# Layer 0's attention steps: two maxima over two banks, the sum of quotients and depthwise on VectorE, the norm on ScalarE

## The chip, the cores and the metric

The kernel runs on one core of a Trainium2 chip. The metric is the device time of one execution in microseconds, as the median of several runs. A core has TensorE (matrix products, its result goes to PSUM, a memory of eight banks for each of 128 partitions), VectorE, ScalarE, GpSimd (which does not take part in PSUM here), SyncE and DMA queues. Each engine works through its own list of instructions in order, and waits at an instruction until what it needs is there.

## What is computed

The reference is a stack of four layers, each with a residual and a group norm before it. Only layer 0 is touched here, on eight images of 128 channels and 56 x 56 pixels:

```python
x = x + L0(gn(x))                      # then layers 1 to 3
# L0, for each image, in 7 x 7 windows of 8 x 8 pixels:
proj = xw @ W_qkv + b_qkv              # q, k, v of 128 channels each
q_win, k_win = q.mean(pixels), k.mean(pixels)
logit = einsum('npc,nqc->npq', q_win * SCALE, k_win)
r_idx = top_k(logit, 4)                # four windows are chosen for each window
attn = softmax(einsum('bmqc,bmkc->bmqk', q_h * SCALE, k_sel))   # 8 heads of 16
o = attn @ v_sel
lepe = depthwise_3x3(v_img) + lepe_b
out = (o + lepe) @ W_o + b_o
```

## The kernel before

All eight images stay on chip as `X`. Layer 0 has 8 x 49 windows; two at a time make a pair, and the 196 pairs are worked off in a pipeline of steps, one loop iteration `p` each, in an order that is written out by hand for TensorE, VectorE, ScalarE and GpSimd. The order within a step is a list of names, `SHORT`, or `LONGER` for a step that also holds a depthwise job.

In step `p` these parts stand on a pair's way, pair `p + 2` entering while pair `p` leaves:

- `scores(p + 2)` (TensorE): the products of the queries, with one head of each two masked, and the chosen keys, for both windows (`o`) and four groups of channels (`g`), into one bank of PSUM for each group (`s0` to `s3` in the pool `ps_s`).
- `maxima` (VectorE, line 577): four, one for each group over 2 x 256 columns, giving the negated maximum of each row. `halve` (GpSimd) splits the result in two bf16 numbers, `flip` (TensorE) turns it, into bank `t2`, and `flipped` (ScalarE) copies it to `nm`.
- `shifted(p + 1)` (TensorE, lines 602 and 612): the transposed scores, four banks `t0` to `t3`; it begins with a product with `nm`, which subtracts the maxima. `exp0` to `exp3` (ScalarE, line 622) make the exponentials.
- `values(p)` (TensorE, line 636): exponentials times values, into bank `s0`. It can only start when `max0` of this step has freed that bank, and the next `scores` needs it back.
- `turned` and `divide` (VectorE, lines 648 to 660) read `values`' result and divide by the sum, into `ot`.
- `join(p - 2)` (GpSimd, line 465): adds the depthwise result to the quotients of the pair before the last. `back(p - 2)` (VectorE, line 471) turns the sum into `outs`.
- `gather` (GpSimd, line 534) copies the chosen keys, `fetch` issues DMAs of the chosen values.

Beside this, each step has room for two jobs, `one` (bank `t0`) and `two` (bank `t1`), and a small one, `light`. A job has a part for TensorE and an end on ScalarE or VectorE. Jobs are `queries` (q, ends on ScalarE, line 415), `keys`, `image` and `pixels` (k and v of the next image, end on ScalarE), `depthwise` (ends on VectorE, lines 449 and 451, and has its input `v` brought by `neighbours`, four DMAs on GpSimd's queue, line 429) and `project` (the output product; ends on VectorE, line 487, with the residual). A planner places them: each has a first step (`ready`) and a last one (`due`), and the earliest due goes first; in a step with depthwise, that is `two`, and it uses bank `t0`. In `SHORT` the end of `one` stands between `exp2` and `exp3`, the end of `two` after `flipped`.

The norm of the next image is done block by block, 49 times in layer 0's loop, in a step's `hooks` at its end, by four instructions of VectorE each (line 292). `hooks` also hold statistics (lines 226 and 496) and sums (line 297), which the planner spreads by weights.

Of the kernel before, what the change touches and what calls it, by code (L numbers as in the profile page):

```python
# [50 lines left out]
def conv_stack_kernel(ctx: ExitStack, tc: tile.TileContext, a: dict, out: bass.AP):  # L51
# [81 lines left out]
    with ExitStack() as l0:  # L133
# [69 lines left out]
        banks = itertools.cycle([(ps, f"{k}{g}") for k, ps in (("s", ps_s), ("t", ps_t)) for g in range(4)])  # L203
# [14 lines left out]
        def measure(b):  # L218
# [28 lines left out]
            def first_root():  # L247

                sd = small.tile([P, 1], F32, name="sd0", tag="sd1")
                nc.scalar.activation(sd, st["pv"], AF.Sqrt, bias=eps)  # L250
                st["r"] = small.tile([P, 1], F32, name="r0_0", tag="r0", bufs=4)
                nc.vector.reciprocal(st["r"], sd)
                st["off"] = small.tile([P, 1], F32, name="off", tag="off", bufs=1)
                nc.vector.tensor_scalar(st["off"], st["gm"], st["r"], -1.0, ALU.mult, ALU.mult)

            def var_end():


                v, t = (small.tile([P, 1], F32, name=f"nr{k}_{b}", tag=f"nr{k}") for k in range(2))
                y = st["r"] = small.tile([P, 1], F32, name=f"r0_{b}", tag="r0", bufs=4)  # L260
                nc.vector.tensor_scalar(v, st["pv"], EPS, None, ALU.add)
                nc.vector.tensor_scalar(t.bitcast(I32), v.bitcast(I32), 1, None, ALU.logical_shift_right)
                nc.vector.tensor_scalar(
                    y.bitcast(I32), t.bitcast(I32), -1.0, float(0x5F3759DF), ALU.mult, ALU.add
                )
                for c in (3.0, 12.0, 768.0):
                    nc.vector.scalar_tensor_tensor(t, y, v, y, ALU.mult, ALU.mult)
                    nc.vector.scalar_tensor_tensor(y, t, -c, y, ALU.add, ALU.mult)
                nc.vector.tensor_scalar(y, y, -1.0 / 8192, None, ALU.mult)

# [188 lines left out]
        def join(p):  # L459


            to = pairs[p]["ot"].rearrange("p k h (q c) -> p k (h q) c", c=FEW)
            for s in sorted({2 * p // NW, (2 * p + 1) // NW}):
                x = lepes[s][:, :, p - s * NW // 2].rearrange("p m (k c) -> p k m c", c=FEW)
                nc.gpsimd.tensor_tensor(to, to, x, ALU.add)
# [93 lines left out]
        def scores(p):  # L559
# [3 lines left out]
                s=[ps_s.tile([P, 2, TOPK * WPX], F32, name=f"s_{p}_{g}", tag=f"s{g}") for g in range(4)],  # L563
                nmax=win.tile([P, 2, 4], F32, name=f"nmax_{p}", tag="nmax"),
            )
            for o in range(2):
                w = wins[2 * p + o]
                for g in range(4):
                    h = slice(g * CL, (g + 1) * CL)
                    nc.tensor.matmul(  # L570
                        s_["s"][g][:, o, :], w["qm"][h].rearrange("p h x -> p (h x)"), w["kw"][h],
# [3 lines left out]
        def maxima(p, g):  # L575
            s_ = pairs[p]
            nc.vector.tensor_reduce(s_["nmax"][:, :, g], s_["s"][g], AX.X, ALU.max, negate=True)  # L577
# [72 lines left out]
        def divide(p):  # L650
# [8 lines left out]
            ot = pairs[p]["ot"] = win.tile([P, 4, 2, 16], F32, name=f"ot_{p}", tag="ot", bufs=2)  # L659
# [12 lines left out]
        made, jobs, hooks, fixed, loose = {}, [], {}, [], []  # L672
# [57 lines left out]
        for f in (image[0], image[1], *pixels[1:]):  # L730
# [3 lines left out]
                     light=(ps_s, "s2"), tails=(ps_s, "s1"))  # L734
# [9 lines left out]
        hook(-1, lambda: neighbours(0, 0))  # L744
# [10 lines left out]
        for b in range(B):  # L755
            for i in range(NBLK):
                q, last = pair_of(b, i * NW), pair_of(b, i * NW + NW - 1)
                if b or i > 1:
                    job(max(pair_of(b, i * NW - NW - 1) - 1, -1), q - 3, lambda b=b, i=i: queries(b, i))
                job(q + 1, q + 1, lambda b=b, i=i: depthwise(b, i), True, LONG)  # L760
                job(last + 3, last + 5, lambda b=b, i=i: project(b, i), name=("project", b, i))
        for b in range(1, B):
# [15 lines left out]
            for i in range(NBLK):  # L778
                fixed.append((at[i], 7, lambda b=b, i=i: once(preparation, b)[6](i)))
                loose.append((at[i], min(at[i] + 2, at[-1]), 6, lambda b=b, i=i: once(preparation, b)[7](i)))  # L780
# [4 lines left out]
            job(at[-1] + 1, due - 2, lambda b=b: once(preparation, b)[4], False, LIGHT, ("means", b))  # L785
            job(at[-1] + 2, due - 1, lambda b=b: once(preparation, b)[5], False, LIGHT, ("route", b),
# [32 lines left out]
        for p, n, f in fixed:  # L819
            weight[p] += n  # L820
            hook(p, f)
# [25 lines left out]
        for k, (name, n) in enumerate(VECTORS):  # L847
# [7 lines left out]
        SHORT = """fetch0 scores shifted gather join max0 max1 values exp0 max2 exp1 max3 halve ahead one light two flip exp2  # L855
            root back turned divide end1 exp3 flipped lit hooks tails end2 fetch1"""
        LONGER = """fetch0 scores shifted gather join max0 max1 values exp0 max2 exp1 max3 halve ahead two exp2 root back
            turned divide end2 flip light one exp3 flipped lit hooks tails end1 fetch1"""
# [18 lines left out]
        for p in range(FIRST, END + 6):  # L877
            one, two, light = (t and t[3]() for t in plan[p])
            acts = {
                "ahead": lambda: ahead(p), "hooks": lambda: every(hooks.get(p, ())), "tails": rest,  # L880
            }
            if 0 <= p + 2 < END:
                acts.update(scores=lambda: scores(p + 2), halve=lambda: halve(p + 2), flip=lambda: flip(p + 2),
                            flipped=lambda: flipped(p + 2))
                for g in range(4):
                    acts[f"max{g}"] = lambda g=g: maxima(p + 2, g)
# [7 lines left out]
            if 0 <= p - 2 < END:  # L894
                acts.update(join=lambda: join(p - 2), back=lambda: back(p - 2))
# [1083 lines left out]
```

## Time and profile before

| | before |
|---|---|
| median of 3 runs | 3294.03 us (3293.73 to 3301.88) |
| the profiled execution | 3306.33 us, span 3304.5 us |
| mean granted clock of TensorE | 0.988 |
| layer 0's steps | about 43 to 1186 us of the span |
| busy from 50 to 1180 us: TensorE, VectorE, ScalarE, GpSimd | 1044, 944, 640, 885 of 1130 us |

Times in the profile are those of one execution. PE is TensorE, PEld its loading of weights, DVE is VectorE, ACT ScalarE, POOL GpSimd, and SP SyncE. In a line on an instruction, `out<-in` are the tiles that it writes and reads. "idle before, releaser" is the time that the engine stood still just before it, and what ended that. A wait is told as who waited for whom: us in total, how often, the longest.

### The profile page before, as it was taken

To read this page: it belongs to the slowest core of one execution; us is meant where nothing else is said; L and a number is where in the kernel's file an instruction comes from. 1 tells how busy PE (TensorE), PEld (TensorE's weight loads), DVE (VectorE), ACT (ScalarE), POOL (GpSimd) and SP (SyncE) were. 2 spreads that over 40 slices of the span, in tenths; PEclk is the share of its full clock that TensorE was granted. 3 is DMA by queue.
4 is the path that set the end of the run, shared out by engine and by line. 5 is a ranking of instruction groups with operands and counts; after the bars stand their busy time and mean duration, and the time that the engine had idled before them with its cause. 6 is when DMAs were issued, how large, how long until landed. Compare 5 with 4: busy or idle time off the path is not lost.

```text
span 3304.5 us, 105617 instructions
## 1 busy us (share of the span) xinstructions
PE 3143.1 (95%) x41230; PEld 2707.2 (82%) x41230; DVE 2327.2 (70%) x6160; ACT 1280.1 (39%) x2432; POOL 1482.2 (45%) x4034
## 2 busy tenths in 40 slices
PE   7999999999998889999999999999999999999998
PEld 5767767776776679999999999999999953499988
DVE  5888888888887866655555555555523257799999
ACT  4555555555565522222111111111112144455654
POOL 4788878877787743333222222222200065322221
PEclk8999999999999999999999999999999999999999
DMA  5566666656566511110000000000022156300001
GB/s 149 129 148 144 145 140 138 149 135 140 128 142 147 114 56 52 49 49 22 1 1 1 1 1 1 1 1 1 21 62 59 52 151 159 87 25 35 30 30 41
DMA packets 196045, 242.76 MB, mean 73 GB/s; under 512 B 46368, under 2 KB 140864, under 8 KB 195536
## 3 DMA queue, kind: packets, MB, share of 16 engines
q0 software_dynamic: 47104, 126.87, 15.9%
q1 hardware_dynamic: 131632, 102.06, 11.5%
q10 hardware_dynamic: 16800, 6.97, 1.0%
q8 instruction: 328, 5.37, 0.7%
q14 instruction: 181, 1.48, 0.2%
HBM read 137.21 MB, written 67.56 MB: 62 GB/s over the span
## 4 chain that ended last, share of the span: by engine, by line
PE 67%; DVE 18%; POOL 5%; issue 5%; ACT 2%; DMA 2%; ACTq 1%; POOLq 1%; DVEq 0%; SPq 0%
PE ps L1112 27%; PE q L1077 9%; PE po L1142 5%; PE po L636 5%; PE t L612 3%; PE pc L1353 3%; PE s L570 3%; PE pi L1047 3%; DVE nmax L577 2%; POOL ks L534 1%; PE pc3b L1599 1%; PE t L602 1%; PE pc L1361 1%; PE pvp L339 1%; DVE u_pc3b L1718 1%
## 5 line engine op out<-in xcount | busy, mean ns | idle before, releaser
L1112 PE MATMUL ps<-hs,w_gates 128*128 128x136 f32 x7680 | 928.8, 279 | 0.0
L1112 PEld LDWEIGHTS ps<-hs,w_gates 128*128 128x128 f32 x7680 | 911.6, 190 | 4.5
L1126 ACT ACTIVATE hs<-v 128x272 f32<-128x272 f32 x538 | 212.3, 404 | 1167.6 <-DVE v L1124 1167.4
L622 ACT ACTIVATE e<-t 128x512 f32<-128x512 f32 x784 | 431.3, 596 | 397.6 <-PE t L612 302.5
L1124 DVE TENSOR_TENSOR v<-ps,g 128x272 f32<-128x272 f32 x538 | 216.4, 411 | 495.5 <-PE ps L1112 409.2
L577 DVE TENSOR_REDUCE nmax<-s 128x2 f32<-128x512 f32 x784 | 485.4, 682 | 78.4 <-PE s L570 76.9
L1065 POOL TENSOR_TENSOR d<-inp 128x136 f32<-128x136 f32 x186 | 87.8, 472 | 789.4 <-DVE inp L1053 789.4
L534 POOL COPY ks<-kT 128x64 f32 x1568 | 293.5, 236 | 142.2 <-PE t L612 93.5
L636 PE MATMUL po<-e,ring 128*32 128x64 f32 x12544 | 250.1, 231 | 23.6 <-DVE nmax L577 13.4
L636 PEld LDWEIGHTS po<-e,ring 128*32 128x32 f32 x12544 | 220.8, 149 | 51.6 <-DVE nmax L577 19.3
L570 PE MATMUL s<-ks,q 32*128 32x256 f32 x3136 | 240.4, 409 | 10.0 <-ACT vp L362 6.1
L612 PE MATMUL t<-q,ks 32*128 32x128 f32 x6272 | 242.0, 275 | 6.4 <-issue 6.4
L612 PEld LDWEIGHTS t<-q,ks 32*128 32x128 f32 x6272 | 223.7, 190 | 11.9 <-issue 8.6
L1599 PE MATMUL pc3b<-vb,u_w2c_t 128*128 128x196 f32 x1152 | 202.2, 338 | 19.9 <-DVE vb L1580 19.9
L1599 PEld LDWEIGHTS pc3b<-vb,u_w2c_t 128*128 128x128 f32 x1152 | 198.7, 195 | 22.2 <-DVE vb L1580 22.0
L1599 PE MATMUL pc3a<-va,u_w1c_t 128*128 128x196 f32 x1152 | 199.9, 334 | 8.1 <-DVE d_pc3a L1616 4.1
L1599 PEld LDWEIGHTS pc3a<-va,u_w1c_t 128*128 128x128 f32 x1152 | 195.1, 193 | 12.0 <-issue 9.7
L1142 PE MATMUL po<-hs,xw 128*128 128x272 f32 x744 | 204.1, 397 | 0.4 <-ACT hs L1126 0.2
L570 PEld LDWEIGHTS s<-ks,q 32*128 32x128 f32 x3136 | 149.9, 188 | 45.5 <-issue 7.6
L1077 PE MATMUL q<-d,mixed 128*128 128x136 f32 x1116 | 160.2, 279 | 0.5 <-DVE g L1091 0.3
L429 POOL DMA_DIRECT2D v<-vimg x224 | 147.6, 665 | 13.7 <-issue 13.3
L1142 PEld LDWEIGHTS po<-hs,xw 128*128 128x128 f32 x744 | 132.0, 190 | 22.4 <-ACT hs L1126 1.0
(307 smaller groups left out, 5394.3 us busy)
## 6 DMA issues: line engine op xcount, KB each, us to landing
v<-vimg POOLq DMA_DIRECT2D x216, 232.0 KB
ring<-vpix SPq DMA_DIRECT2D x1176, 32.0 KB
kept<-g SPq DMA_DIRECT2D x56, 272.0 KB, 2.1
g<-kept SPq DMA_DIRECT2D x56, 272.0 KB, 2.7
xkeep<-X POOLq DMA_DIRECT2D x56, 224.0 KB
vimg<-vrow POOLq DMA_DIRECT2D x108, 116.0 KB
out_dram<-u_pc3b SPq DMA_DIRECT2D x31, 392.0 KB, 2.4
vpix<-vp POOLq DMA_DIRECT2D x42, 256.0 KB
```

The costliest lines, as they stand in the source:

```text
L534: nc.gpsimd.tensor_copy(kw[:, t : t + 1, :], ks[b][:, bass.ds(at, 1), :])
L570: nc.tensor.matmul(s_["s"][g][:, o, :], w["qm"][h].rearrange("p h x -> p (h x)"), w["kw"][h], start=True, stop=True,)
L577: nc.vector.tensor_reduce(s_["nmax"][:, :, g], s_["s"][g], AX.X, ALU.max, negate=True)
L612: nc.tensor.matmul(s_["t"][g][:, o, c], w["kw"][h, c * P : (c + 1) * P], w["qm"][h].rearrange("p h x -> p (h x)"), start=False, stop=(o == ...
L622: nc.scalar.activation(s_["e"][g], s_["t"][g], AF.Exp)
L636: mm = nc.tensor.matmul(po[g * CL : (g + 1) * CL, h, :, o], flat[:, at : at + 8 * CL - 7 : 8], s_["e"][g][:, o, c, h * WPX : (h + 1) * WPX ...
L1077: nc.tensor.matmul(q[n // 3][:, n % 3], w, x, start=True, stop=True)
L1112: nc.tensor.matmul(ps[f][:, i], whh[:, k, m * P : (m + 1) * P], prev[k // 2][:, (s - 1) % 2, k % 2].rearrange("p c b -> p (c b)"), start=( ...
L1124: nc.vector.tensor_tensor(v[:, i : i + n], ps[f][:, i : i + n], x, ALU.add)
L1126: nc.scalar.activation(to, x, AF.Tanh)
L1142: nc.tensor.matmul(po, wout[:, k, :], hs[k // 2][:, :, k % 2], start=(k == 0), stop=(k == KH - 1))
L1599: nc.tensor.matmul(bank[:, half].rearrange("p (y x) -> p y x", x=H4), u[:, dy, k, :], v[:, k, i * RB + dy : i * RB + dy + RB, :], start=(d ...
```

## The change

- The scores of a pair go to two tiles of two banks (`s0`, `s1`) instead of four tiles of one. Two maxima over 2 x 2 x 256 columns take the place of four. The light job uses `s1` instead of `s2`. Before the loop, the products go round in 6 tiles instead of 8.
- `join` is done by VectorE, and `join` and `back` follow `divide` of the same pair in the same step; `ot` needs one buffer.
- The norm of the loop is done by ScalarE, at the begin of the step after (`early`), with `off = -mean * r` as its bias, which `var_end` now makes.
- Around this, jobs move: `queries` is due where it is ready, five steps ahead of its first pair; `depthwise` is a step earlier; `project` is ready two steps earlier and due one; sums, means and route are a step later.

```diff
-        banks = itertools.cycle([(ps, f"{k}{g}") for k, ps in (("s", ps_s), ("t", ps_t)) for g in range(4)])
+        banks = itertools.cycle([(ps_s, "s0"), (ps_s, "s1")] + [(ps_t, f"t{g}") for g in range(4)])
...
+                st["off"] = small.tile([P, 1], F32, name=f"off_{b}", tag="off")
+                nc.vector.tensor_scalar(st["off"], st["gm"], y, -1.0, ALU.mult, ALU.mult)
...
-                nc.gpsimd.tensor_tensor(to, to, x, ALU.add)
+                nc.vector.tensor_tensor(to, to, x, ALU.add)
...
-                s=[ps_s.tile([P, 2, TOPK * WPX], F32, name=f"s_{p}_{g}", tag=f"s{g}") for g in range(4)],
+                s=[ps_s.tile([P, 2, 2, TOPK * WPX], F32, name=f"s_{p}_{k}", tag=f"s{k}") for k in range(2)],
...
-                        s_["s"][g][:, o, :], w["qm"][h].rearrange("p h x -> p (h x)"), w["kw"][h],
+                        s_["s"][g // 2][:, g % 2, o], w["qm"][h].rearrange("p h x -> p (h x)"), w["kw"][h],
...
-        def maxima(p, g):
+        def maxima(p, k):
             s_ = pairs[p]
-            nc.vector.tensor_reduce(s_["nmax"][:, :, g], s_["s"][g], AX.X, ALU.max, negate=True)
+            to = s_["nmax"][:, :, 2 * k : 2 * k + 2].rearrange("p o g -> p g o")
+            nc.vector.tensor_reduce(to, s_["s"][k], AX.X, ALU.max, negate=True)
...
-            ot = pairs[p]["ot"] = win.tile([P, 4, 2, 16], F32, name=f"ot_{p}", tag="ot", bufs=2)
+            ot = pairs[p]["ot"] = win.tile([P, 4, 2, 16], F32, name=f"ot_{p}", tag="ot", bufs=1)
...
-                     light=(ps_s, "s2"), tails=(ps_s, "s1"))
+                     light=(ps_s, "s1"), tails=(ps_s, "s1"))
...
-        hook(-1, lambda: neighbours(0, 0))
+        hook(-2, lambda: neighbours(0, 0))
...
-                    job(max(pair_of(b, i * NW - NW - 1) - 1, -1), q - 3, lambda b=b, i=i: queries(b, i))
-                job(q + 1, q + 1, lambda b=b, i=i: depthwise(b, i), True, LONG)
-                job(last + 3, last + 5, lambda b=b, i=i: project(b, i), name=("project", b, i))
+                    job(max(q - 5, -1), q - 5 + (i < 4 and not b), lambda b=b, i=i: queries(b, i))
+                job(q, q, lambda b=b, i=i: depthwise(b, i), True, LONG)
+                job(last + 1, last + 4, lambda b=b, i=i: project(b, i), name=("project", b, i))
...
-                fixed.append((at[i], 7, lambda b=b, i=i: once(preparation, b)[6](i)))
-                loose.append((at[i], min(at[i] + 2, at[-1]), 6, lambda b=b, i=i: once(preparation, b)[7](i)))
+                early.setdefault(at[i] + 1, []).append(lambda b=b, i=i: once(preparation, b)[6](i, True))
+                loose.append((at[i] + 1, min(at[i] + 3, at[-1] + 1), 6, lambda b=b, i=i: once(preparation, b)[7](i)))
...
-        SHORT = """fetch0 scores shifted gather join max0 max1 values exp0 max2 exp1 max3 halve ahead one light two flip exp2
-            root back turned divide end1 exp3 flipped lit hooks tails end2 fetch1"""
-        LONGER = """fetch0 scores shifted gather join max0 max1 values exp0 max2 exp1 max3 halve ahead two exp2 root back
-            turned divide end2 flip light one exp3 flipped lit hooks tails end1 fetch1"""
+        SHORT = """fetch0 early scores shifted gather max0 values exp0 max1 exp1 halve ahead one light two flip exp2
+            root turned divide join back end1 exp3 flipped lit hooks tails end2 fetch1"""
+        LONGER = """fetch0 early scores shifted gather max0 values exp0 max1 exp1 halve ahead two exp2 root
+            turned divide end2 join back flip light one exp3 flipped lit hooks tails end1 fetch1"""
...
-            if 0 <= p - 2 < END:
-                acts.update(join=lambda: join(p - 2), back=lambda: back(p - 2))
+            if 0 <= p < END:
+                acts.update(join=lambda: join(p), back=lambda: back(p))
```

More of the change, by code (lines that the diff above doesn't have):

```diff
@@ L252, in first_root @@
                 nc.vector.reciprocal(st["r"], sd)
-                st["off"] = small.tile([P, 1], F32, name="off", tag="off", bufs=1)
+                st["off"] = small.tile([P, 1], F32, name="off0", tag="off")
                 nc.vector.tensor_scalar(st["off"], st["gm"], st["r"], -1.0, ALU.mult, ALU.mult)
@@ L671, in conv_stack_kernel @@
         LIGHT, ONE, LONG = range(3)
-        made, jobs, hooks, fixed, loose = {}, [], {}, [], []
+        made, jobs, hooks, early, loose = {}, [], {}, {}, []
         def once(make, b):
@@ L784, in conv_stack_kernel @@
                 job(at[min(i + 1, NBLK - 1)] + 1, due - 1, lambda b=b, i=i: once(preparation, b)[3][i])
-            job(at[-1] + 1, due - 2, lambda b=b: once(preparation, b)[4], False, LIGHT, ("means", b))
-            job(at[-1] + 2, due - 1, lambda b=b: once(preparation, b)[5], False, LIGHT, ("route", b),
+            job(at[-1] + 2, due - 2, lambda b=b: once(preparation, b)[4], False, LIGHT, ("means", b))
+            job(at[-1] + 3, due - 1, lambda b=b: once(preparation, b)[5], False, LIGHT, ("route", b),
                 [("means", b)])
@@ L818, in conv_stack_kernel @@
             loose.append((p + 1, p + 1 + (b < B - 1), 5, lambda b=b, i=i: measured(b, i)))
-        for p, n, f in fixed:
-            weight[p] += n
-            hook(p, f)
         for b, (name, n) in itertools.product(range(1, B), (("mean", 9), ("var", 13), ("means", 5), ("route", 10))):
@@ L879, in conv_stack_kernel @@
             acts = {
-                "ahead": lambda: ahead(p), "hooks": lambda: every(hooks.get(p, ())), "tails": rest,
+                "ahead": lambda: ahead(p), "hooks": lambda: every(hooks.get(p, ())), "tails": rest, "early": lambda: every(early.get(p, ())),
             }
@@ L884, in conv_stack_kernel @@
                             flipped=lambda: flipped(p + 2))
-                for g in range(4):
-                    acts[f"max{g}"] = lambda g=g: maxima(p + 2, g)
+                for k in range(2):
+                    acts[f"max{k}"] = lambda k=k: maxima(p + 2, k)
             if 0 <= p + 1 < END:
```

## The prediction

> **What bounds the kernel now.** I read the page first, then the busy time of the stretch in which layer 0 runs its 196 steps (50 to 1180 us), then what the engines waited for in it, and last the timeline of single steps.
>
> ```profile
> PE 3143.1 (95%) x41230; PEld 2707.2 (82%) x41230; DVE 2327.2 (70%) x6160; ACT 1280.1 (39%) x2432; POOL 1482.2 (45%) x4034
> ```
>
> ```profile
> core 0: us, PE busy (x) PEld busy (x) DVE busy (x) ACT busy (x) POOL busy (x), PEclk, DMA share, GB/s
> ...
> 50.00:1180.00 1130.00, 1044.13 (x25691) 797.22 (x25689) 944.25 (x2386) 639.62 (x1235) 885.33 (x2826) 0.99 0.60 137
> ```
>
> The 70% of VectorE is an average: in layer 0 it is busy 84% of the time, GpSimd 78%, TensorE 92%, ScalarE 57%. Nothing outside layer 0 is edited, so everything is decided in these 1130 us. The start of `shifted` moves from 43.1 to 1175.1 us in 195 steps: 5.8 us a step. TensorE idles 86 us in all, 0.44 us a step: that is the most that any relief of the other engines can return while TensorE's work is the same.
>
> The waits, of TensorE and then of VectorE:
>
> ```profile
> PE po L636 <- DVE nmax L577: 13.4, 23, 1.9
> PE t L602 <- ACT q L415: 9.0, 20, 0.6
> PE flip L589 <- POOL halves L584: 7.7, 12, 2.0
> ```
>
> ```profile
> DVE outs L471 <- POOL ot L465: 75.2, 89, 2.6
> DVE nmax L577 <- PE s L570: 62.3, 77, 6.3
> ```
>
> The longest wait of VectorE (75.2 us: `back` for GpSimd's `join`) goes away with the change. But TensorE's own longest wait is already for the maxima, since `values` writes into the bank that the first maximum frees. One step in which VectorE was on time (start us, us, instruction):
>
> ```profile
> 475.04 1.15 PE L570 MATMUL s<-ks,q 32*128 32x256 f32 x16
> ...
> 476.01 0.55 PE L602 MATMUL t<-nm,ones 2*128 2x512 bf16 x4
> ...
> 476.21 2.48 DVE L577 TENSOR_REDUCE nmax<-s 128x2 f32<-128x512 f32 x4 [0.48 <-PE s L570]
> 476.23 1.22 PE L612 MATMUL t<-q,ks 32*128 32x128 f32 x32
> ...
> 477.38 1.24 PE L636 MATMUL po<-e,ring 128*32 128x64 f32 x64
> ```
>
> The maximum starts 0.20 us after `shifted` does, and `values` can start 1.2 to 1.4 us after it. One maximum of one bank (0.68 us) fits in with half a microsecond to spare.
>
> **The change, part by part.** The groups with the prices (busy us, mean ns | idle before it); the last two are of the whole layer:
>
> ```profile
> L577 DVE TENSOR_REDUCE nmax<-s 128x2 f32<-128x512 f32 x776 | 480.5, 682 | 63.8 <-PE s L570 62.3
> ...
> L471 DVE STREAM_TRANSPOSE outs<-ot 128x128 f32<-128x128 f32 x194 | 59.3, 306 | 75.9 <-POOL ot L465 75.2
> L660 DVE TENSOR_TENSOR ot<-turned,rden 128x128 f32<-128x128 f32 x195 | 57.2, 293 | 6.7
> ...
> L292 DVE TENSOR_SCALAR xw<-X,gm,r 128x112 f32<-128x112 f32 x196 | 54.9, 362 | 0.0
> ...
> L236 DVE COPY gm<-pm 128x1 f32<-128x1 f32 x7 | 1.0, 143 | 0.0
> ```
>
> ```profile
> L465 POOL TENSOR_TENSOR ot<-ot,lep 128x128 f32<-128x128 f32 x224 | 101.6, 454 | 6.3 <-DVE ot L660 2.8 <-DVE lep L451 1.4
> ...
> L290 ACT ACTIVATE xw<-X,off,r 128x112 f32<-128x112 f32 x12 | 4.6, 474 | 0.5 <-DVE off L254 0.5
> ```
>
> Maxima. An almost empty instruction that reads PSUM takes 0.14 us (L236), so 512 columns cost 0.54 and a maximum over 1024 columns 1.22 us (estimate). The trace has no such instruction: 1.15 to 1.30 as bounds, the upper from the slope of the two transposes of PSUM, 417 ns for 256 columns and 717 for 512. In a row, four take 2.48 us now; two would take about 2.3. VectorE saves 0.16 us a step, 31 us in all. Trace Analysis of the Trainium skill, "Optimizing Scalar/DVE Operations", says that an instruction on PSUM costs VectorE about 125 ns beside its data: by that VectorE would save 0.25 us a step, 49 us, and the sum below would be some 3 us lower, as VectorE would be 0.09 us earlier. The same section says that where an engine is not saturated but makes others wait, smaller pieces let work end sooner; this speaks against the change.
>
> Join. L660, the same size, takes 293 ns; each of the row turned, reciprocal, quotient, sum, turn needs the one before, and in the timeline such a successor starts 0.03 us after its predecessor's end. 224 sums of 0.32 and 0.11 us more per quotient, which no longer overlaps with its successor: 93 us on VectorE. GpSimd loses 102 us.
>
> Norm. 49 blocks of four: VectorE loses 55 us (4 take 1.07), ScalarE gains 49 x 1.53 = 75 us (4.6 us for 12, L290). ScalarE idles 1.2 to 2.3 us before the first exponential of a step (the timeline around 600 us), so I take 0 for it. It costs where the step before ends with queries and an image; see the rivals. The extra `off`, 7 of 0.15 us, is nothing.
>
> VectorE's row then shrinks by 0.16 + 0.28 (norm) + 0.39 (wait for `join`) - 0.48 (sums) = 0.35 us a step, and it will be earlier at its maxima by about that.
>
> Now the term that decides. `values` may start when the first maximum has ended; the trace shows 0.05 us from that end to the matmul. After the change the first maximum covers groups 0 and 1, so it starts when the sixth instead of the fifth of eight products is there (0.1 us later; eight take 0.97) and ends 0.54 us later. From the timeline I took, for the 149 steps between 140 and 1020 us that can be separated, the start of the first maximum and the end of `shifted`, and summed what `values` would wait. With 0.68 us this gives 10.5 us for the maxima as they are. With 1.22 us: 33 us if VectorE is 0.35 us earlier, 47 if it is no earlier, 27 if it is never late, 17 if besides the 0.1 us is not there. Times 194/149 steps, less what is paid now: **+29 us**, bounds +8 and +47.
>
> What comes back: TensorE's waits for GpSimd's `halves` (7.7 us; the cast stood behind `join`), and for `project` and `depthwise` on VectorE (4.4 and 3.0 in the same view): **-10** of these 15; bounds 0 and -30, because weight loads waited 40 us for `halves` too, mostly behind a matmul still running.
>
> Order of jobs. The plan now takes queries always as the first job of a step: 54 times instead of 28 first and 26 second. As second job their ScalarE part (1.35 us) held bank t1 past the next `shifted`: 9.0 us in the view above, gone: **-9**. As first job it stands between the third and fourth exponential, and the next `shifted` waits for `nm` behind it. From one `values` end to the next this makes 0.6 (exponential) + 0.4 (rest of the product) + 1.34 + 0.56 + 0.37 + 0.06 + 2.34 (`shifted` and `values`) = 5.7 us, whatever else TensorE has to do. Before, the light steps held depthwise alone (46; by the starts of `shifted` 5.24 us in the mean, where 4.63 of work lie in the step above). Now 28 hold queries alone, at 5.7 with 4.6 of work, 20 an image alone, and 50 depthwises share a step. Per seven steps TensorE loses 2 x 0.6 in light steps now, and after 1.1 with queries and some 0.4 with an image (estimate: as before, less `join`): +0.3 in 7, **+7** over 165 steps; bounds -10 and +25.
>
> Earlier `join`, `back`, `project`: two steps less after the last pair (the last project began 1185.2, could at 1182.5): **-3**. DMAs: `neighbours` is issued one step earlier, as is the depthwise that needs it; GpSimd's queue, through which it goes, is shorter: 0. The means, variances and routes (28 steps) read PSUM on VectorE behind `join` and `back` now, 0.5 us later, and scores wait for them (3.7 us in the waits of before): 0, as `back` no longer waits; 8 us if each costs 0.3. Fewer banks before the loop: PE waits there for ScalarE already, 0.
>
> Sum: 29 - 10 - 9 + 7 - 3 = +14. The profiled execution took 3306.33 us (span 3304.5), 0.4% over the runs' median of 3294.03; on the median's scale 3308.
>
> **Rivals.**
>
> (1) VectorE's row is the limit and its relief decides: faster, from the point where VectorE is so early that `values` waits less than before. For it: 84% busy, 75.2 us of waiting gone, and nmax starts only 77 of 196 times because it waited for scores; otherwise VectorE itself was late. Against: only 24.5 of the 86 us idle of TensorE end on VectorE. If half of the idle (43) returns and `values` costs only its lower bound plus 10 us elsewhere, 25 us are won: 3269. Range 3235 to 3284.
>
> (2) The two cancel: 3284 to 3304.
>
> (3) ScalarE's early norm becomes a bound in the steps after queries with an image: copy of `vrow` 0.66 and norm 1.53 stand before the first exponential, which frees t0 for the first job. From `nm` to that release pass 0.66 + 1.53 + 0.55 (exponential) + 0.06 = 2.8 us, where `shifted` and `values` take 2.34: 0.45 us lost in each of 18 such steps, 8 us. With the wait of `values` at its upper bound (+18 over the term) the sum is 14 + 8 + 18 = +40: 3334.
>
> (4) The change doesn't do what it says: excluded; the order of the built instructions shows 392 maxima less on VectorE, 224 sums more, and 196 products of norm on ScalarE.
>
> **How the numbers follow.** The measurement can tell 0.3%, 10 us, from no change. The forecast (values wait for the long maximum, slower) with rival 3 has 0.50, of it 0.08 for rival 3; no change 0.20; rival 1 has 0.30. The likeliest case's own range is 3304 to 3335. The range over all leaves out the ends of rivals 1 and 3: 3258 to 3345.
>
> **What would show it.** In the waits of TensorE after, `po <- nmax` at 35 to 60 us instead of 13.4, in every second step; VectorE's wait for `ot` gone, its busy time in the stretch near 940 (944 - 31 - 55 + 93 = 951); a maximum of 1.22 us; ScalarE near 715. `t L602 <- q` gone, `t <- nm` longer. Wrong would be: `values` starting within 1.5 us of `shifted` in most steps, with `po <- nmax` under 15 us; then VectorE's earlier start carried it, and the time falls to rival 1.

## The result: 3337.67 us after, and the profile after

| | before | after |
|---|---|---|
| median of 4 runs | 3294.78 us (3293.73 to 3301.88) | 3337.67 us (3335.17 to 3338.65) |
| ratio to before | | 1.0124, interval 1.0107 to 1.0142 |
| profiled execution, span | 3306.33, 3304.5 us | 3338.18, 3336.3 us |
| granted clock | 0.988 | 0.987 |
| first to last `shifted` (195 steps) | 43.1 to 1175.1 us, 5.805 a step | 42.6 to 1205.9 us, 5.966 a step |

Slower, by 43 us between the medians (35 to 47 by the interval). The two profiled executions differ by 31.9 us only, since the one before was 12 us over its median. Of these, 31.3 lie in the 195 steps; from the last `shifted` to the end of the span it is 2129.4 us before and 2130.4 after. So the whole difference is made in layer 0's loop. Of the executions behind the ratios below, two stand far off the rest, one of d1_two (7276.95 us) and one of d5_due (3358.78 us), and are left out of the ratios.

The first section of the page after, and the row of the windows for 50 to 1180 us:

```profile
PE 3148.4 (94%) x41230; PEld 2702.4 (81%) x41230; DVE 2341.0 (70%) x5803; ACT 1351.2 (40%) x2628; POOL 1394.7 (42%) x3810
```

```profile
core 0: us, PE busy (x) PEld busy (x) DVE busy (x) ACT busy (x) POOL busy (x), PEclk, DMA share, GB/s
50.00:1180.00 1130.00, 1018.73 (x25006) 770.57 (x25010) 936.95 (x1986) 697.05 (x1406) 783.99 (x2554) 1.00 0.56 135
```

TensorE gets through 25006 matmuls in these 1130 us, where it got through 25691: 2.7% fewer. VectorE is at 937 us (944 before), GpSimd at 784 (885); only ScalarE has more to do, 697 (640), and it is far from full. From the first to the last `shifted`, TensorE is busy for the same time, 1044.4 us before and 1044.8 after, and stands still for 87.6 us before and 118.5 after. So the time went into waits. TensorE's, from 50 to 1210 us (us in total, times, the longest):

```profile
PE po L639 <- DVE nmax L580: 31.0, 65, 1.3
PE flip L592 <- POOL halves L587: 19.3, 22, 2.0
PE t L605 <- DVE X L489: 16.6, 29, 1.7
PE t L605 <- ACT nm L596: 14.3, 35, 1.0
```

Two of these stood lower in the list before (50 to 1180 us):

```profile
PE t L602 <- ACT nm L593: 6.6, 19, 1.0
...
PE t L602 <- DVE X L487: 4.4, 13, 0.4
```

Against before: `values` for the maxima +17.6 (from 13.4), `flip` for the halves +11.6 (from 7.7), `shifted` for the residual `X` of `project` +12.2 (from 4.4), `shifted` for `nm` +7.7 (from 6.6). The wait for queries' `q` (9.0) is gone. VectorE's two largest after, and its wait for `values` before:

```profile
DVE turned L651 <- PE po L639: 93.0, 195, 3.7
DVE nmax L580 <- PE s L572: 72.4, 98, 8.5
```

```profile
DVE turned L648 <- PE po L636: 19.1, 20, 3.6
```

This is the line that points to the cause. Before, VectorE waited 75.2 us for GpSimd's `join` and 19.1 for `values`, 94.3 together. Now it waits 93.0 us for `values`, in every step. Nothing of that wait was saved; only its name and its place changed.

The prices in layer 0, from the groups of VectorE and of ScalarE (busy us, mean ns | idle before it):

```profile
L580 DVE TENSOR_REDUCE nmax<-s 128x4 f32<-128x1024 f32 x388 | 456.1, 1218 | 72.9 <-PE s L572 72.4
L651 DVE STREAM_TRANSPOSE turned<-po 128x256 f32<-128x256 f32 x195 | 87.7, 450 | 93.0 <-PE po L639 93.0
L467 DVE TENSOR_TENSOR ot<-ot,lep 128x128 f32<-128x128 f32 x222 | 64.3, 289 | 6.6
```

```profile
L292 ACT ACTIVATE xw<-X,off,r 128x112 f32<-128x112 f32 x196 | 80.2, 490 | 19.4 <-issue 18.6 <-DVE X L489 0.5 <-DVE r L269 0.3
```

And one stretch of the timeline (start us, us, instruction), with a depthwise and a project in the same step:

```profile
775.19 0.45 DVE L651 STREAM_TRANSPOSE turned<-po 128x256 f32<-128x256 f32 x1 [1.59 <-PE po L639]
...
776.36 0.72 DVE L453 STREAM_TRANSPOSE lep<-plep 128x512 f32<-128x512 f32 x1
...
777.11 0.29 DVE L467 TENSOR_TENSOR ot<-ot,lep 128x128 f32<-128x128 f32 x1
...
777.44 0.31 DVE L473 STREAM_TRANSPOSE outs<-ot 128x128 f32<-128x128 f32 x1
...
777.67 1.02 DVE L489 SCALAR_TENSOR_TENSOR X<-py,bo,X 128x112 f32<-128x112 f32 x4
...
777.87 0.38 PE L605 MATMUL t<-nm,ones 2*128 2x512 bf16 x1
778.61 1.21 DVE L580 TENSOR_REDUCE nmax<-s 128x4 f32<-128x1024 f32 x1
...
778.75 0.39 PE L605 MATMUL t<-nm,ones 2*128 2x512 bf16 x3 [0.51 <-DVE X L489]
```

VectorE stands still for 1.59 us, then has its whole step to do at once: turn, reciprocal, quotient, depthwise, sum, turn back, residual. TensorE reaches `shifted` at 777.87 and waits 0.51 us for the residual to free a bank; the next maximum starts 0.74 us after `shifted`, not 0.2.

### The profile page after: what moved, and what is told of

It is laid out like the page before. It is cut to its first block, busy times and chain, and to the rows that moved or that the text cites. A ratio compares the mean times of both kernels' runs of the same rounds, so it can differ in the third digit from the quotient of the medians.

```text
span 3336.3 us, 105314 instructions
## 1 busy us (share of the span) xinstructions
PE 3148.4 (94%) x41230; PEld 2702.4 (81%) x41230; DVE 2341.0 (70%) x5803; ACT 1351.2 (40%) x2628; POOL 1394.7 (42%) x3810
## 4 chain that ended last, share of the span: by engine, by line
PE 70%; DVE 19%; ACT 3%; issue 3%; DMA 2%; POOL 2%; ACTq 1%; POOLq 0%; SPq 0%; DVEq 0%
PE ps L1112 27%; PE q L1077 9%; PE po L639 6%; PE po L1142 5%; DVE nmax L580 4%; PE pc L1353 4%; PE s L572 4%; PE pi L1047 3%; PE t L615 2%; DMA ring<-vpix 1%; PE pc L1361 1%; PE pc3b L1599 1%; PE plep L445 1%; PE pvp L341 1%; PE pq L412 1%
## 5 line engine op out<-in xcount | busy, mean ns | idle before, releaser
L580 DVE TENSOR_REDUCE nmax<-s 128x4 f32<-128x1024 f32 x392 | 460.8, 1218 | 87.3 <-PE s L572 86.8
L651 DVE STREAM_TRANSPOSE turned<-po 128x256 f32<-128x256 f32 x196 | 88.2, 450 | 93.9 <-PE po L639 93.9
```

Of the source, the lines that this page charges most:

```text
L580: nc.vector.tensor_reduce(to, s_["s"][k], AX.X, ALU.max, negate=True)
```

## The experiments

Each ratio is to runs of the kernel before on the same chip; their median was 3301.8 to 3304.0 us there. Versions that ran on different chips are therefore compared by their ratios.

### One piece of the change undone

**u1_four: the kernel after with four maxima of one bank.**

```diff
-            nc.vector.tensor_reduce(to, s_["s"][k], AX.X, ALU.max, negate=True)
+            nc.vector.tensor_reduce(s_["nmax"][:, :, g], s_["s"][g], AX.X, ALU.max, negate=True)
```

> The changed kernel with four maxima over one bank each, all else as changed. Theory A (values waits for the long first maximum): TensorE's wait for nmax falls from 31 us to under 8, halves come no later, and 25 to 35 us of the 43 come back (3303 to 3313). Rival B (VectorE's row of sums is too long): the row grows by 0.13 us a step, so at most 8 us come back or up to 10 us more are lost (3329 to 3348).

3335.64 us, 1.0101 (1.0076 to 1.0126). TensorE's waits from 50 to 1210 us:

```profile
PE flip L591 <- POOL halves L586: 38.6, 40, 2.5
PE t L604 <- DVE X L489: 16.7, 39, 1.2
```

The wait of `values` for the maxima fell from 31.0 to 5.1 us, and the wait for the halves rose from 19.3 to 38.6. Hardly anything of the loss came back: the long maximum alone is not its cause. VectorE's wait for `values` fell too, from 93.0 to 54.9 us, so that wait in itself is no price either. Trace Analysis of the Trainium skill, "Optimizing Scalar/DVE Operations", says that smaller pieces may let work end sooner where an engine that is not saturated makes others wait. Here `values` got its bank sooner, and the step did not end sooner; `halve` needs all four maxima anyway.

**u2_join: the kernel after with the sum on GpSimd and `back` two steps late, as before; project as before; depthwise still one step early.**

```diff
-                nc.vector.tensor_tensor(to, to, x, ALU.add)
+                nc.gpsimd.tensor_tensor(to, to, x, ALU.add)
...
-                job(last + 1, last + 4, lambda b=b, i=i: project(b, i), name=("project", b, i))
+                job(last + 3, last + 5, lambda b=b, i=i: project(b, i), name=("project", b, i))
```

> The changed kernel with the sum of quotients and depthwise on GpSimd again, two steps later, and project two steps later. Theory A: under 10 us either way (3328 to 3348), VectorE's wait for GpSimd comes back with some 50 to 75 us and the wait for nmax stays above 25. Rival B: the wait of the shifted products for project's end (t <- X, 16.6 us) falls to 5, halves too, 20 us or more come back (3318 or less).

3328.7 us, 1.0078 (1.0054 to 1.0103): about a third comes back. The wait for `X` fell from 16.6 to 2.8 us, but the halves took 37.4 us, and VectorE again waits for GpSimd's `ot`, 127.2 us. The depthwise stays early in this run; d7_plan below shows what that costs with the sum on GpSimd.

**u3_norm: the kernel after with the norm on VectorE, at the end of the step before.**

```diff
-                early.setdefault(at[i] + 1, []).append(lambda b=b, i=i: once(preparation, b)[6](i, True))
+                fixed.append((at[i], 7, lambda b=b, i=i: once(preparation, b)[6](i)))
```

> The changed kernel with the norm on VectorE in a step's hooks again. Theory A: VectorE is later by 55 us of work in all, so values waits longer: 10 to 25 us more (3347 to 3362). Rival C (ScalarE's early norm holds up the first exponential, 11 us of TensorE's waits): 5 to 15 us come back (3322 to 3332).

3342.27 us, 1.0116 (1.0092 to 1.014). No gain: the norm on ScalarE is not the cause. The wait for the maxima rose to 43.1 us and that for `X` to 22.1, while VectorE is busy 1007 us in the loop instead of 961.

**u4_ask2: the kernel after with queries as the second job of a step that has no image.**

```diff
+            if one and one[6] in asks and not (two and two[4]):
+                one, two = two, one
```

> The changed kernel with queries as the second job wherever the step has no image, so that their end on ScalarE stands behind nm. Theory A: nothing to do with it, within 8 us (3329 to 3346). Rival D (queries as first job make a loop of 5.7 us through ScalarE): the 28 steps that hold queries alone fall from 5.9 to near 5.0 us, and 15 to 25 us come back (3312 to 3322).

3343.22 us, 1.0121 (1.0097 to 1.0144). The waits move with the jobs: `t <- q` is back (11.7 us) and `t <- nm` falls to 5.3. The 20 steps that hold queries alone fall from 6.05 to 5.51 us in the mean, and 19 steps with a depthwise and `pixels` rise from 6.34 to 7.06. The time as a whole does not move.

### One piece done alone

**d1_two: the kernel before with two maxima over two banks.**

```diff
-            nc.vector.tensor_reduce(s_["nmax"][:, :, g], s_["s"][g], AX.X, ALU.max, negate=True)
+            to = s_["nmax"][:, :, 2 * k : 2 * k + 2].rearrange("p o g -> p g o")
+            nc.vector.tensor_reduce(to, s_["s"][k], AX.X, ALU.max, negate=True)
```

> The kernel before with the scores in two tiles of two banks and two maxima, nothing else. Theory A (values waits for the long maximum): nmax waits rise from 13 to 35 us or more and the kernel is 20 to 30 us slower than before. Theory F (VectorE's row from maximum to maximum sets a step; four maxima or one long one with its wait for values make the same row): within 10 us of before.

3305.27 us, 1.0013 (0.9998 to 1.0027). TensorE's largest wait from 50 to 1180 us:

```profile
PE po L637 <- DVE nmax L578: 37.9, 70, 2.4
```

24.5 us more than the 13.4 of before, in 47 more steps, near what the prediction had; and the time moves by 4 us, of which the interval leaves 0 open. The added wait did not become added time.

**d2_norm: the kernel before with the early norm on ScalarE.**

```diff
-                fixed.append((at[i], 7, lambda b=b, i=i: once(preparation, b)[6](i)))
+                early.setdefault(at[i] + 1, []).append(lambda b=b, i=i: once(preparation, b)[6](i, True))
```

> The kernel before with the norm on ScalarE at a step's begin, nothing else. Theory F: VectorE's row is 0.28 us a step shorter, 10 to 30 us faster than before. Rival C (ScalarE's early norm holds up the first exponential): 0 to 15 us slower.

3300.07 us, 0.9999 (0.9986 to 1.0012): nothing, where theory F expected 10 to 30 us less.

**d5_due: the kernel before with queries due five steps ahead.**

```diff
-                    job(max(pair_of(b, i * NW - NW - 1) - 1, -1), q - 3, lambda b=b, i=i: queries(b, i))
+                    job(max(q - 5, -1), q - 5 + (i < 4 and not b), lambda b=b, i=i: queries(b, i))
```

> The kernel before with queries due where they are ready, five steps ahead, so that they come first among the jobs and the others are paired anew; no instruction more or less. Rival E (pairing): 20 us or more slower, steps that hold queries alone take 5.7 us or more. Theory F: within 8 us of before.

3307.05 us, 1.0017 (1.0 to 1.0033): about 5 us.

**d3_join: the kernel before with the sum and `back` on VectorE behind the pair's own `divide`, depthwise one and project two steps earlier.**

```diff
-            root back turned divide end1 exp3 flipped lit hooks tails end2 fetch1"""
+            root turned divide join back end1 exp3 flipped lit hooks tails end2 fetch1"""
```

> The kernel before with the sum on VectorE in one row with turned and divide, depthwise one step and project two steps earlier; norm, maxima and queries as before. Theory F: the row takes 0.43 us a step more and loses a wait of 0.39, so it is 0 to 20 us slower. Rival E (the cost lies in how the plan of the change pairs the jobs): within 8 us, as queries keep their due.

3330.75 us, 1.0092 (1.0063 to 1.0121), some 30 us, more than either theory expected. Most of the loss is there, without the maxima, the norm and the queries. TensorE's wait for `X`, from 50 to 1210 us:

```profile
PE t L602 <- DVE X L487: 20.1, 40, 1.4
```

This version joins four things: another engine, another place in the row, the earlier depthwise, the earlier project. The next runs take them apart.

### Engine, place and step

**d6_engine: the kernel before with the sum on VectorE, still two steps late, in the gap ahead of `back` and `turned`.**

```diff
-                nc.gpsimd.tensor_tensor(to, to, x, ALU.add)
+                nc.vector.tensor_tensor(to, to, x, ALU.add)
...
-            root back turned divide end1 exp3 flipped lit hooks tails end2 fetch1"""
+            root join back turned divide end1 exp3 flipped lit hooks tails end2 fetch1"""
```

> The kernel before with the sum on VectorE, still two steps late and right before back, so that it fills the time in which VectorE waits for values; plan as before. Theory F (the row behind VectorE's wait for values is what costs): no loss, 0 to 20 us faster than before, as 0.39 us a step of waiting for GpSimd go and 0.32 of work come. Theory H (VectorE has too much to do, wherever the sum stands): 15 us or more slower.

3298.44 us, 0.998 (0.9971 to 0.999): the engine alone costs nothing; it gains a little.

**d7_plan: the kernel before with the depthwise, and the `neighbours` of the first, one step earlier.**

```diff
-        hook(-1, lambda: neighbours(0, 0))
+        hook(-2, lambda: neighbours(0, 0))
...
-                job(q + 1, q + 1, lambda b=b, i=i: depthwise(b, i), True, LONG)
+                job(q, q, lambda b=b, i=i: depthwise(b, i), True, LONG)
```

> The kernel before with depthwise one step earlier, nothing else; the planner pairs other jobs with it. Theory F: within 8 us of before. Theory G (pairing depthwise with other jobs heaps GpSimd's DMA issues and VectorE's ends in one step): 15 to 30 us slower, with TensorE's wait for halves at 25 us or more.

3341.51 us, 1.0114 (1.0097 to 1.0131): one move costs 38 us. A step with queries alone, in the timeline of this run:

```profile
798.75 1.93 POOL L429 DMA_DIRECT2D v<-vimg  x3
...
800.67 0.79 POOL L214 DMA_DIRECT2D vpix<-vp  x1
...
801.44 0.56 POOL L74 DMA_DIRECT2D X<-in_x_dram  x1
802.00 0.54 POOL L549 DMA_DIRECT2D ring<-vpix  x1
...
802.53 1.46 POOL L534 COPY ks<-kT 128x64 f32 x8
...
803.96 0.97 POOL L465 TENSOR_TENSOR ot<-ot,lep 128x128 f32<-128x128 f32 x2
...
804.88 0.21 POOL L583 CAST halves<-nmax 128x8 bf16<-128x8 f32 x1
...
805.47 0.29 PE L589 MATMUL flip<-ident,halves 128*128 128x128 bf16 x2 [1.97 <-POOL halves L584]
```

GpSimd works through 6.1 us of DMA issues, copies and sums without a pause before it gets to the halves, and TensorE waits 1.97 us. Over the loop `flip` waits 55.7 us for the halves, in 59 steps (7.7 before); in 38 of them, with 45 of the 56 us, the cast did not start when the maxima were ready, but when GpSimd was free. The granted clock of this execution was 0.982 instead of 0.988, and TensorE is busy 1056 us in the loop instead of 1044, so some 11 of the 38 us may be the clock's.

**u8_gap: the kernel after with the sum and `back` on VectorE two steps late ahead of `turned`, depthwise and project as before.** Two maxima, early norm and early queries stay.

```diff
-                job(q, q, lambda b=b, i=i: depthwise(b, i), True, LONG)
-                job(last + 1, last + 4, lambda b=b, i=i: project(b, i), name=("project", b, i))
+                job(q + 1, q + 1, lambda b=b, i=i: depthwise(b, i), True, LONG)
+                job(last + 3, last + 5, lambda b=b, i=i: project(b, i), name=("project", b, i))
...
-            root turned divide join back end1 exp3 flipped lit hooks tails end2 fetch1"""
+            root join back turned divide end1 exp3 flipped lit hooks tails end2 fetch1"""
```

> The changed kernel (two maxima, norm on ScalarE, sum on VectorE, queries due early) with sum and back two steps late, between the maxima and turned, and depthwise and project due as before. Theories F and G: 3290 to 3310, the 43 us are back. Theory H: still 3320 or more.

3300.99 us, 0.9994 (0.9985 to 1.0004): all is back, with these three pieces of the change still in.

**d8_both: d6_engine and the norm on ScalarE, placed ahead of `fetch0`.** Maxima, queries, depthwise and project are as before.

```diff
-        SHORT = """fetch0 scores shifted gather join max0 max1 values exp0 max2 exp1 max3 halve ahead one light two flip exp2
-            root back turned divide end1 exp3 flipped lit hooks tails end2 fetch1"""
+        SHORT = """early fetch0 scores shifted gather max0 max1 values exp0 max2 exp1 max3 halve ahead one light two flip exp2
+            root join back turned divide end1 exp3 flipped lit hooks tails end2 fetch1"""
```

> The kernel before with the sum on VectorE as in d6 and the norm on ScalarE ahead of that step's first DMA. Theory F: VectorE's row is 0.28 us shorter than in d6, so 10 to 40 us faster than before. Theory H: VectorE does 944 + 72 - 55 us, no faster than before.

3287.46 us, 0.9947 (0.9931 to 0.9964): faster than both kernels, the best version found.

### Why: six more runs

**p1_alone: d7_plan, but from step 23 on the planner holds back any job not yet due when the depthwise comes.**

```diff
+            if long and one and 23 <= p < one[0]:
+                one = None
             if long:
                 two = long
```

> The kernel before with its depthwise one step earlier, as in the run that moved only that, but from step 23 on the planner holds back any other job that is not yet due when the depthwise comes, so that the depthwise is alone in 45 of the 166 steps from 15 to 180 (40 before, 6 with the move alone). Theory of pairing (two full jobs in the depthwise's step make that step long and leave another step with one short job, on whose short row GpSimd's transfers fall): 3300 to 3312 us, TensorE's waits for the halves at the flip under 25 us (55.7 with the move alone). Theory of the step itself (the depthwise needs its neighbours and its tables a step too early, whatever shares its step): 3335 to 3345. In between, 3315 to 3330, would leave both with a part.

3304.01 us, 1.0003 (0.999 to 1.0017): the loss of d7_plan is gone. The wait for the halves is 32.2 us, above the expected 25.

**p2_late: the kernel before with the next image's norm and its jobs one step later.**

```diff
-            at = [pair_of(b - 1, i * NW) - 5 for i in range(NBLK)]
+            at = [pair_of(b - 1, i * NW) - 4 for i in range(NBLK)]
```

> The kernel before, depthwise where it was, but the norm of the next image and the jobs that follow from it (keys, image, pixels, means, route) are ready one step later. The depthwise then shares its step with keys or pixels 27 times of 48 (8 before, 41 with the depthwise moved), and 22 images and no queries are alone. Theory of pairing: the loss goes with the shared steps, 19 more against 33 more that cost 38 us: about +22, 3320 to 3335. Theory of the step itself: no depthwise moved, so 3300 to 3310. Theory of GpSimd's queue: as pairing, with the flip's waits for the halves at 25 to 45 us.

3313.27 us, 1.0037 (1.0027 to 1.0048), halves 23.2 us: sharing costs something without a moved depthwise, but half of what was expected.

**p3_gps: d7_plan with the sum as in d6_engine.**

```diff
-                nc.gpsimd.tensor_tensor(to, to, x, ALU.add)
+                nc.vector.tensor_tensor(to, to, x, ALU.add)
...
-            root back turned divide end1 exp3 flipped lit hooks tails end2 fetch1"""
+            root join back turned divide end1 exp3 flipped lit hooks tails end2 fetch1"""
```

> The kernel with only the depthwise one step earlier (3341.5 us), and the sum of quotients and depthwise by VectorE in the gap ahead of its turns instead of GpSimd: 97 us of work less on GpSimd, nothing else moved. Theory of GpSimd's queue (the depthwise's new place crowds the issues of transfers ahead of the halves, and the flip waits for them): the flip's waits for the halves fall from 55.7 to under 25 us, the time to 3300 to 3315. Theory of pairing without the queue (TensorE's and ScalarE's own rows are too long where two jobs meet): the halves fall as well, but other waits take their place, and the time stays at 3328 to 3340.

3293.69 us, 0.9975 (0.9962 to 0.9988). The early depthwise, which costs 38 us with the sum on GpSimd, costs nothing with the sum on VectorE, although it shares its steps as in d7_plan. So d7_plan's loss, but for the clock's part, is GpSimd's: shared steps and GpSimd's sum together make it, and either cure is enough. The expected wait was missed, though:

```profile
PE flip L589 <- POOL halves L584: 40.0, 43, 2.4
PE po L636 <- DMA ring<-vpix: 12.0, 20, 1.3
```

40 us of waiting for the halves (under 25 was expected) stand in a kernel that is faster than the one before, where it was 7.7. The size of one wait does not tell the time. TensorE's whole standstill in the loop is 89.1 us here and 87.6 before: other waits gave way.

**p4_afteralone: the kernel after with the rule of p1_alone.**

```diff
+            if long and one and 23 <= p < one[0]:
+                one = None
```

> The kernel after, with the same rule from step 23 on: the depthwise keeps its earlier step, but alone in 45 of 166 steps (2 in the kernel after). Everything else of the change stays: two maxima, the norm by ScalarE, the sum by VectorE in the row. Theory of pairing: most of the 43 us come back, 3295 to 3315. Theory of the step itself, or of the sum standing in the row right before its turns: 3325 to 3342.

3341.92 us, 1.0124 (1.0098 to 1.015): nothing is back. What costs in the kernel after is not the sharing. Again one wait took another's place: for the halves 0.7 us (19.3 after), for the maxima 67.4 (31.0).

**p5_rowlate: d3_join with the project at its old steps.** Against p3_gps it differs in one thing: the sum and `back` stand behind the pair's own `divide`, instead of two steps late ahead of `turned`.

```diff
-                job(last + 1, last + 4, lambda b=b, i=i: project(b, i), name=("project", b, i))
+                job(last + 3, last + 5, lambda b=b, i=i: project(b, i), name=("project", b, i))
```

> The kernel before with the sum by VectorE in the row behind its own pair's turn and division, and the depthwise one step earlier, as in the run at 3330.8 us that had the project two steps earlier too; here the project keeps its old steps. The run that had the same earlier depthwise with the sum by VectorE two steps late, in the gap ahead of the turns, took 3293.7. Theory of the row (VectorE first waits for its pair's values, and only then does the sum and the turns back, so that nothing fills the wait and all that stands behind them on VectorE comes later): 3322 to 3335 us, VectorE's waits for the values over 35 us. Theory of the project (its earlier place is what costs): 3293 to 3305, and the same waits cost nothing.

3317.61 us, 1.006 (1.0041 to 1.0078), between what the two theories expected and nearer to that of the row. The place in the row costs 24 us (28 by the ratios, 0.0085 x 3303). From 50 to 1210 us:

```profile
DVE turned L648 <- PE po L636: 31.2, 47, 4.0
```

```profile
PE flip L589 <- POOL halves L584: 46.0, 54, 2.4
PE po L636 <- DVE nmax L577: 18.4, 37, 1.7
...
PE t L602 <- DVE X L487: 4.0, 10, 0.8
```

VectorE's wait for `values` was 31.2 us, a little under the expected 35 (16.6 in p3_gps). What stands behind it comes later: VectorE's first maximum begins over 0.5 us after `shifted` in 66 of 193 steps, in p3_gps in 47, and `values` waits 18.4 us for it instead of 7.3. Against d3_join the earlier project makes 0.0032 more, about 11 us, but the two intervals overlap.

**p6_gap1: the kernel after, whole, but the sum and `back` are those of the pair before and stand ahead of `turned`; the project may come at `last + 2`.**

```diff
-                job(last + 1, last + 4, lambda b=b, i=i: project(b, i), name=("project", b, i))
+                job(last + 2, last + 4, lambda b=b, i=i: project(b, i), name=("project", b, i))
...
-            root turned divide join back end1 exp3 flipped lit hooks tails end2 fetch1"""
+            root join back turned divide end1 exp3 flipped lit hooks tails end2 fetch1"""
...
-            if 0 <= p < END:
-                acts.update(join=lambda: join(p), back=lambda: back(p))
+            if 0 <= p - 1 < END:
+                acts.update(join=lambda: join(p - 1), back=lambda: back(p - 1))
```

> The kernel after, whole, but the sum and the turns back are those of the pair before, one step late, and stand ahead of the step's turns on VectorE, and the project may come one step later for it (last + 2 instead of last + 1). Two maxima, the norm by ScalarE, the early depthwise and the early queries stay. Theory of the row: 3290 to 3308 us, VectorE's waits for the values from 93 to under 30 us. Theory that the cause is elsewhere in the planning (queries, depthwise paired with project): 3325 to 3340, though the waits shrink.

3300.97 us, 0.9996 (0.9984 to 1.0009): the whole loss is gone. VectorE's waits and TensorE's, from 50 to 1180 us:

```profile
DVE nmax L580 <- PE s L572: 122.8, 151, 8.5
DVE turned L651 <- PE po L639: 26.6, 38, 3.3
```

```profile
PE po L639 <- DVE nmax L580: 28.0, 75, 1.2
PE t L605 <- ACT nm L596: 20.6, 37, 1.0
PE flip L592 <- POOL halves L587: 8.7, 12, 1.4
...
PE t L605 <- DVE X L489: 3.8, 7, 1.1
```

VectorE's wait for `values` falls from 93.0 to 26.6 us, and it is ahead of the scores in 151 steps instead of 98: it now waits for new scores, with its older work done. `X` and the halves, the two waits that had grown by 23.8 us, fall by 12.8 and 10.6. The wait for the long maximum stays (28.0 against 31.0), though the loss is gone. The loop is 33.8 us shorter than in the kernel after (1129.5 against 1163.3), at a granted clock in it of 0.996 against 0.994. Of these, 19.8 are standstill of TensorE and 14.0 its busy time, and no run shows why the same products took less. A step with a project in the timeline:

```profile
761.19 0.28 DVE L467 TENSOR_TENSOR ot<-ot,lep 128x128 f32<-128x128 f32 x1
...
761.50 0.31 DVE L473 STREAM_TRANSPOSE outs<-ot 128x128 f32<-128x128 f32 x1
...
761.73 0.41 DVE L651 STREAM_TRANSPOSE turned<-po 128x256 f32<-128x256 f32 x1
...
762.62 1.05 DVE L489 SCALAR_TENSOR_TENSOR X<-py,bo,X 128x112 f32<-128x112 f32 x4
...
764.15 0.55 PE L605 MATMUL t<-nm,ones 2*128 2x512 bf16 x4
```

The sum begins while `values` still runs (to 761.44 by its line in the timeline), and the sum and the turn back are done ahead of `turned`; the residual starts 0.89 us after `turned` and is done before `shifted`. In the step shown of the kernel after, it started 2.48 us after `turned`: 1.59 more, some 0.6 of it for the sum and the turn back and the rest for the depthwise of that step.

Two edits are in this run, and its plan puts no project into a depthwise's step (24 in the kernel after). p4_afteralone took that sharing away with the sum left in its place, and gained nothing; p5_rowlate and p3_gps differ in the place alone, 24 to 28 us. So the place is shown for the larger part, and the project one step earlier stays as a possible 11 us of the 43.

## Why the prediction was right and wrong

The direction was right and the time within the range over all, but outside the likeliest case's own, 3304 to 3335. The size was not right, 14 us predicted and 43 measured, and the term that was to decide was not the one that did: the long maximum, +29 us in the sum, is worth some 4 us alone. What made the kernel slower is a piece that the sum counted as a gain. So the right direction was luck.

**The step that failed** is in the part on the join: "VectorE's row then shrinks by 0.16 + 0.28 (norm) + 0.39 (wait for `join`) - 0.48 (sums) = 0.35 us a step, and it will be earlier at its maxima by about that." It adds up VectorE's work and waits, whatever their place in the row, and counts the 0.39 us as gained time. But `turned` needs `values`, and with the wait for `join` taken away VectorE arrived at `turned` earlier and waited there: 75.2 + 19.1 us became 93.0. What had been done while `values` ran, the turn back, and the new sum besides, now came after it. That place, put at nothing, is worth 0.0085 of the time, some 28 us, between p5_rowlate and p3_gps, which have the same plan; with the project one step earlier it is 0.0128, some 42 us, between the kernel after and p6_gap1. The length of VectorE's wait is not the price: it is 54.9 us in u1_four and 46.4 in d3_join, which keep most of the loss. Nor was VectorE much earlier at its maxima: the first of a step began over 0.5 us after `shifted` in 53 of 193 steps before, in 48 of 189 after, and in 15 of 193 in p6_gap1, which does the same work.

**What comes back, -10**, had the wrong sign: the waits for the halves and for `project`'s residual went up by 11.6 and 12.2 us. The place of the sum does not make them by itself. Behind the pair's own `divide`, the wait for `X` is 20.1 us with the early project (d3_join) and 4.0 without (p5_rowlate), and the wait for the halves is 0.7 us where the depthwise seldom shares its step (p4_afteralone). The early queries raise the wait for `X` too, to 17.7 us in d5_due, with the sum on GpSimd. In all 22 steps in which `flip` still waited for the halves, GpSimd itself was behind.

**Values and the long maximum, +29.** As a wait it was within the term's bounds: +17.6 us, 65 times, though less than the 35 to 60 us "in every second step" that were to show it. The instruction takes 1.218 us (1.22 estimated) and two in a row 2.36 (2.3). As a term of the sum it was worth almost nothing: d1_two pays 24.5 us of it for 4 us of time, p6_gap1 pays 28.0 and is as fast as before, u1_four spares it and is hardly faster. The forecast added a wait to the time without asking what would be waited for next if it were not there.

**Queries.** `t <- q` went as said (-9), `t <- nm` grew as said (6.6 to 14.3). A step with queries alone takes 6.05 us in the mean, 5.7 predicted. u4_ask2 undoes the order of the jobs and d5_due does the due times alone: nothing, and 5 us, of which the interval leaves 0 open.

**Depthwise and `neighbours`, 0.** The reason given was that GpSimd's queue "is shorter", and it held: with GpSimd's sum the same step costs 38 us (d7_plan), without it nothing (p3_gps). The prediction named the right cover; it did not say what the move costs where that cover is missing.

**The small terms.** Norm on ScalarE: 80.2 us for 75 predicted, free as said (u3_norm, d2_norm). Tail: 3 us expected, none seen. VectorE 937 for 951, ScalarE 697 for 715: the longer loop puts fewer steps into the window.

**Rivals.** Rival 1, the relief of VectorE that decides, is real when the sum keeps its place: d6_engine gains 0.2%, d8_both 0.5%. Of rival 3 the wait can be seen: first jobs wait 11.3 us for an exponential (`pvp` 6.7, `plep` 4.6; before, `plep` 2.8), but u3_norm, which takes its reason away, is no faster. That rival 3's sum, 3334, comes near the measured time is chance.

**What stays open**: how the 43 us divide. By the ratios, p3_gps to p5_rowlate (the place) is 0.0085, p5_rowlate to d3_join (the project) 0.0032, and d3_join to the kernel after (maxima, norm and queries) again 0.0032; for each of the last two the intervals of the two runs overlap, and in u8_gap the last three pieces cost nothing. Open, too, is which other waits give way where one grows: p3_gps and p1_alone lose nothing with 40.0 and 32.2 us of waiting for the halves, and TensorE's whole standstill in the loop is 89.1 and 87.1 us there, 87.6 before.

## What to carry to other kernels

When an edit takes a wait away from an engine, look at the next thing in its order that depends on another engine: if that is not earlier, the wait only moves, and all work that used to fill it is put behind it. So place work that depends on old results ahead of an engine's wait for new ones; a lag of one step, for the sum and for the project, was worth some 42 us here with the same work. And a wait's microseconds are a price only if one run shows that taking it away moves the time.

## What the runs showed of the hardware

- VectorE's maximum over PSUM took 682 ns for 512 columns and 1218 for 1024; four of the one in a row took 2.48 us, two of the other 2.36. So each instruction spared saved 0.06 us.
- GpSimd's issue of one DMA occupied it for 0.52 to 0.80 us in the kernel after (four for a depthwise's `neighbours` took 2.6 us). In the step shown of d7_plan, a cast of 0.21 us stood behind 6.1 us of such issues, copies and sums.
- ScalarE's own DMA issue took 0.49 us in the mean. With such an issue just ahead of the norm, ScalarE stood still for 18.6 us in 17 places before the norms of the kernel after; in d8_both, with the norm ahead of the issue, for 0.0. No run shows what that alone is worth in time.
